# A batch's routing next to its layer norm in the first stage, and two bias additions on GpSimd in the middle stage

## The chip, the cores and the metric

One Trainium2 chip, one core. The metric is the time of one execution in microseconds on the device; a kernel's time is the median over its runs. All data are float32. In the profile PE is TensorE (PEld its weight loads), DVE is VectorE, ACT is ScalarE, POOL is GpSimd, and SP is SyncE, which only issues DMAs (SPq is its queue).

## The reference

The input x has 8 batches of 1024 tokens of 256 features. Three blocks follow each other, each with a residual: a feed-forward block taken by half, attention, and the same feed-forward block once more with the same weights.

```python
x = x + 0.5 * ffn(layernorm(x))
x = x + attn(layernorm(x))
x = x + 0.5 * ffn(layernorm(x))

def ffn(x):                      # 16 experts, inner size 128; shared expert of 2 x 128
    s    = softmax(x @ gate_w.T)             # 16 scores, plus gate_b for the choice
    keep = best 2 of 4 groups of experts     # by the sum of a group's two best
    w, idx = best 2 experts within keep      # w: the scores of the chosen
    y = sum over the 2 of  w * ((silu(x @ We1 + be1) * (x @ We3 + be3)) @ We2 + be2)
    z = (silu(x @ ws1 + bs1) * (x @ ws3 + bs3)) @ ws2 + bs2      # shared expert
    return y + z

def attn(x):                     # linear attention, 16 heads of 16
    q, k, v = split(x @ w_qkv.T);  q, k = relu(q), relu(k)
    z   = 1 / (sum over tokens of k, times q, + eps)
    out = ((v^T k) q) * z
    return out @ w_proj.T + b_proj
```

Two biases matter here: `bs2`, which the kernel keeps halved and broadcast as `hb2`, and `b_proj`, kept as `bpj`. Each is a row of 256 that is added to every token.

## The kernel before

One batch of x is a tile of 128 partitions by 8 x 256 (NT = 8 token tiles); NB = 2 halves of HT = 4 token tiles each. The work has five stages.

1. **First stage, 0 to about 249 us.** For rounds r = 0 to 8: `normed(0, r)` makes the layer norm of batch r (statistics L253 on DVE, scaling L270 on ACT) and transposes it (L283 on PE, copies L286 on ACT). `route(…, r-1)` routes the batch before: gating matmul L323 and transposes L332 on PE, a chain of some thirty small DVE operations from `sm` L339 over `sel` L406 to `cw` L433, in the middle of it the matmuls L416 (tile `prk`) that count tokens by expert, and then on POOL 16 indirect DMAs per batch (L467), which scatter the rows of tokens to the experts' lists `xs_d` in DRAM, with small `L456` and `L461` operations among them. `shared_units(r-2)` computes the shared expert of the batch two back: hidden layer L796 on PE (tiles `p_s`), L800 on ACT, L801 on DVE; output L815 on PE (`py_s`) and L819 on DVE, which adds to x. `add_bias` (L806, DVE) adds `hb2` to half a batch of x first.
2. **Expert blocks of the first feed-forward layer, about 249 to 522 us**, in a written-out order: rows `xg` are loaded by SP from `xs_d` (L654), transposed (L678, tile `pxg`), run through the experts (L699 to L731) and scattered to `ys_d` by POOL (L736). The routing of batch 7, beyond its first two steps, and parts of the shared expert of batch 7 (`late`) run behind these blocks. In between, x tiles are moved to and from `xk_d` in DRAM.
3. **Middle stage, about 522 to 1000 us.** In round r: `begin(r)` adds the experts' outputs to x (`combine`, L856 on DVE, operands loaded by SP) and makes the layer norm for attention; `attention(r-1)` adds `bpj` to the whole batch (L867, DVE, 128 x 2048), then q and k (L877, L881, L882), the sums `pgs` (L885), `gk` (L892, ACT), `dg` (L896, DVE), `pks` (PE), `ksb` (L905, ACT), `qk` (L920, DVE) and `den`, and the projection `pp` (L954, PE), which L958 on DVE adds to x; `finish(r-2)` makes the second feed-forward block's layer norm and routing, with scatters again on L467. The shared expert of that block is computed here for the last batches only.
4. **Expert blocks of the second feed-forward layer, about 1000 to 1271 us**, as in 2.
5. **The end, to 1376 us**: shared expert and output of the remaining batches, with `add_bias` on DVE as in the first stage.

The order: the engines run their own instruction streams, each in order. In stages 1, 3 and 5 a scheduler places each engine's instructions; it gives precedence to what is emitted first. The emission is by Python generators, and `run` takes one step of each in turn:

```python
run(normed(0, r), routing, shared_units(xs[s], xnTs.pop(s), f"s0_{s}"))   # s = r - 2
```

In the last two rounds this differs: in round 7 the routing of batch 6 is run alone before the others; in round 8 only two steps of batch 7's routing are run. `xpool` holds 4 batches of x at a time, so batches 0 to 4 (all but the last LATE = 3) are stored to `xk_d` as they finish. In the middle stage x is loaded again, and from batch 3 on this is done by SP one round ahead.

SP issues the loads of expert weights and rows in order. One of the loads, of the experts' output biases (L236), uses a buffer that the shared expert's last hidden matmul must have left; the first `xg` load of the expert blocks stands behind it.

Of the kernel before, what the change touches and what calls it, by code (L numbers as in the profile page):

```python
# [15 lines left out]
ALU = mybir.AluOpType  # L16
# [3 lines left out]
P = 128  # L20
# [6 lines left out]
def macaron_kernel(  # L27
# [18 lines left out]
    nc = tc.nc  # L46
    B, N, D = x.shape
# [4 lines left out]
    NT = N // P  # L52
# [4 lines left out]
    NB = N // TB  # L57
# [9 lines left out]
    HT = TPB  # L67
# [38 lines left out]
    def load_x(b, src, pieces=1):  # L106
        xt = xpool.tile([P, NT, D], F32, tag="x", name=f"x_{b}")
        n = NT // pieces
        for i in range(pieces):
            nc.sync.dma_start(  # L110
                out=xt[:, i * n : (i + 1) * n, :], in_=src[:, i * n : (i + 1) * n, :]
            )
        return xt

    xs = {0: load_x(0, x_v[0], 4)}
# [17 lines left out]
    hb2 = const.tile([P, D], F32, name="hb2")  # L133
    nc.sync.dma_start(out=hb2[:], in_=bs2.partition_broadcast(P))
    nc.vector.tensor_scalar(hb2[:], hb2[:], 0.5, None, ALU.mult)
    bpj = const.tile([P, D], F32, name="bpj")
# [22 lines left out]
    def ramp(n, first, step, name):  # L159
# [36 lines left out]
        base=0, channel_multiplier=1,  # L196
# [21 lines left out]
    def half(tag, shape, name, dtype=F32):  # L218

        if tag == "xnT":  # L220
            n = shared_room["turn"] % NXT
            shared_room["turn"] += 1
            if n < NXT - NXT_KEPT:
                return shared_room["pool"].tile(
                    shape, dtype, tag=tag, name=name, bufs=NXT - NXT_KEPT
                )
            return big.tile(shape, dtype, tag=tag, name=name, bufs=NXT_KEPT)
        return big.tile(shape, dtype, tag=tag, name=name, bufs={"xn": 8, "k": 2}[tag])
# [80 lines left out]
    def new_base(which):  # L309
        base = rp.tile([P, E], F32, tag="base", name=f"base_{which}", bufs=2)  # L310
        nc.gpsimd.tensor_copy(base[:], eoff[:])
        return base
# [167 lines left out]
    def counts(base, name, unit):  # L480

        cnt = rp.tile([1, E], F32, tag="cnt", name=f"cnt_{name}", bufs=2)
        nc.vector.tensor_tensor(cnt[:], base[0:1, :], eoff[0:1, :], ALU.subtract)
        nc.vector.tensor_scalar(cnt[:], cnt[:], 1.0 / unit, None, ALU.mult)
        return cnt

    def whole(cnt, name, op):

        more = half("xn", [1, E, MB], f"more_{name}")
        nc.vector.tensor_tensor(  # L490
            more[:], cnt[:].unsqueeze(2).to_broadcast([1, E, MB]),
            iblk[0:1, 0:MB].unsqueeze(1).to_broadcast([1, E, MB]), op,
        )
        nblk = rp.tile([1, E], F32, tag="nb", name=f"nb_{name}")
        nc.vector.tensor_reduce(nblk[:], more[:], axis=AX.X, op=ALU.add)
        return nblk
# [48 lines left out]
    def first_map(base, which):  # L545


        name = f"{which}a"
        cnt = counts(base, name, RB)
        nc.vector.tensor_scalar(cnt[:], cnt[:], -1.0, None, ALU.add)  # L550
        nblk = whole(cnt, name, ALU.is_ge)
        maps = []
        for _ in listed(nblk, None, name, maps, RB):
            pass
        end = rp.tile([1, E], F32, tag="done", name=f"done_{name}", bufs=2)
        nc.vector.tensor_tensor_scan(end[:], ones[0:1, 0:E], nblk[:], 0.0, ALU.mult, ALU.add)
        nc.vector.tensor_tensor(end[:], end[:], nblk[:], ALU.subtract)
        nc.vector.tensor_scalar(end[:], end[:], -1.0, float(N1), ALU.mult, ALU.add)
        nc.vector.tensor_scalar(end[:], end[:], 0.0, None, ALU.max)
        nc.vector.tensor_tensor(end[:], end[:], nblk[:], ALU.min)  # L560
        nc.vector.tensor_scalar(end[:], end[:], float(NR), None, ALU.mult)

        fill = half("xn", [P, DR], f"fill_{which}")
        nc.gpsimd.memset(fill[:], 0.0)
        nc.gpsimd.memset(fill[:, D : D + 1], float(SKIP))
        return maps, end, fill
# [27 lines left out]
    def behind(routing, base, which, maps, done, fill):  # L594

        for _ in range(7):
            next(routing)
            yield
        other = second_map(base, which, maps, done)
        last = next(other)  # L600
        yield
        fills = fill_up(last, fill)
        live = True
        while live:
            live = False
            for g in (routing, routing, other, fills):
                if next(g, StopIteration) is not StopIteration:
                    live = True
                    yield
# [192 lines left out]
            h[:], p3[:], bc[:, NS + s : NS + s + 1], h[:], ALU.add, ALU.mult  # L802
        )

    def add_bias(xh):
        nc.vector.tensor_tensor(  # L806
            xh, xh, hb2[:].unsqueeze(1).to_broadcast([P, HT, D]), ALU.add
        )

    def outputs(xh, hs, name):  # L810
# [17 lines left out]
    def half_of(xt, nb):  # L828
        return xt[:, nb * HT : (nb + 1) * HT, :]

    def shared_units(xt, xnT, name, late_bias=False):
        for nb in range(NB):
            xh = half_of(xt, nb)
            if not late_bias:
                add_bias(xh)
            hs = []
            for s in range(NS):
                if late_bias and nb == 0:
                    hs.append(spare(f"hs_{name}_{nb}_{s}"))
                else:  # L840
                    hs.append(
                        mid.tile([P, TB], F32, tag="u2", name=f"hs_{name}_{nb}_{s}", bufs=3)
                    )
                hidden(xnT[nb], s, hs[s], f"{name}_{nb}")
                yield
            if late_bias:
                add_bias(xh)
            yield from outputs(xh, hs, f"{name}_{nb}")

    def combine(which, b, xt):  # L850

        for j in range(0, NT, 2):
            for k in range(K):
                y = mid.tile([P, 2, D], F32, tag="u1", name=f"y_{which}_{b}_{j}_{k}", bufs=4)
                nc.sync.dma_start(out=y[:], in_=ys_v[k, b, :, j : j + 2, :])
                nc.vector.tensor_tensor(  # L856
                    xt[:, j : j + 2, :], xt[:, j : j + 2, :], y[:], ALU.add
                )
            yield


    def attention(b, xt, axn, axnT):
# [1 line left out]
        pgs = [  # L864
            ps_h.tile([P, D + 1], F32, tag="p3", name=f"pgs_{b}_{c}") for c in range(NC)
        ]
        nc.vector.tensor_tensor(  # L867
            xt[:], xt[:], bpj[:].unsqueeze(1).to_broadcast([P, NT, D]), ALU.add
        )
        for j in range(NT):  # L870
            nb, t = divmod(j, HT)
            if t == 0:
# [88 lines left out]
    def part(gen, n):  # L961

        for _ in range(n):
            next(gen, None)
            yield

    def run(*gens):

        live = [g for g in gens if g is not None]
        while live:  # L970
            for g in list(live):
                if next(g, StopIteration) is StopIteration:
                    live.remove(g)

    xns, xnTs = {}, {}

    def normed(which, b):

        xns[b], xnTs[b] = [], []
        parts = NT // 2 if (which, b) == (0, 0) else 1  # L980
        yield from layernorm(xs[b], f"f{which}_{b}", xns[b], DR, parts)
        yield from transposed(xns[b], f"f{which}_{b}", xnTs[b])


    LATE = 3
    base = new_base(0)
    for r in range(B + 1):
        if r == 1:
            load_late_weights()
        if 2 <= r + 1 < B:  # L990
            xs[r + 1] = load_x(r + 1, x_v[r + 1])
        s = r - 2
        routing = None
        if r >= 1:
            routing = route(base, 0, r - 1, xns.pop(r - 1), xnTs[r - 1], r == B)
        if r == B:
            maps, done, fill = first_map(base, 0)
            steps = behind(routing, base, 0, maps, done, fill)
        if r == B - 1:
            run(routing)  # L1000
        run(
            normed(0, r) if r < B else None,
            routing if r < B else part(routing, 2),
            shared_units(xs[s], xnTs.pop(s), f"s0_{s}") if s >= 0 else None,
        )
        if 0 <= s < B - LATE:
            nc.sync.dma_start(out=xk_d[s][:], in_=xs.pop(s)[:])
    tc.no_sync_barrier()

    def park(b, j):  # L1010
# [22 lines left out]
        moves += [partial(fetch, b, j) for j in range(NT)]  # L1033

    s = B - 1
    late = shared_units(xs[s], xnTs.pop(s), f"s0_{s}", True)
    blocks(maps, 0, steps, by_block(moves), partial(steps_of, late, NS))
    for b in range(B - LATE, B - 1):
        xs.pop(b)
# [4 lines left out]
    base = new_base(1)  # L1044
    axns, last = {}, []

    def begin(b):
        yield from combine(0, b, xs[b])
        axns[b] = ([], [])
        yield from layernorm(xs[b], f"a{b}", axns[b][0], D + 1)  # L1050
        yield from transposed(axns[b][0], f"a{b}", axns[b][1])
# [15 lines left out]
    for r in range(B + 2):  # L1067
        if LATE <= r + 1 < B - 1:
            xs[r + 1] = load_x(r + 1, xk_d[r + 1])
        s = r - 3  # L1070
# [11 lines left out]
    s = B - 1  # L1082
# [6 lines left out]
    xh, hs, left, todo = {}, {}, {}, list(range(2, B - LATE))  # L1089
# [35 lines left out]
    maps, done, fill, routing = last  # L1125
# [49 lines left out]
    with tc.manual_schedule():  # L1175
# [10 lines left out]
        for h in range(NH):  # L1186
# [8 lines left out]
            b, nb = own[h]  # L1195
# [68 lines left out]
```

## Time and profile before

| | |
|---|---|
| median of 6 runs | 1371.29 us (1360.54 to 1384.53) |
| the profiled execution | 1377.62 us, span 1375.9 us, granted clock 0.941 |
| PE busy | 1184.0 us, 86% of the span |
| DVE busy | 885.8 us, 64% |
| POOL busy | 581.5 us, 42% |
| ACT busy | 540.4 us, 39% |
| scatters L467 on POOL | 256, mean 1031 ns |
| `hb2` adds L806 on DVE | 32 in the kernel, 128 x 1024, median 1218 ns |
| `bpj` adds L867 on DVE | 8, 128 x 2048, median 2277 ns |

The shares are means over stages that differ, so the view of slices and the windows of one stage matter more than the totals. Idle time of an engine is listed under the group that came after it, with what ended it. POOL in particular idles for long stretches in the middle stage, waiting for the routing weights `cw` (L433).

### The profile page before, as it was taken

The page shows a single profiled execution, that of the slowest core. Times are in us where ns is not written, and L with a number is a line of the kernel's source. Part 1 is how long each engine was busy: PE and PEld are TensorE (multiplying, and loading weights), DVE is VectorE, ACT ScalarE, POOL GpSimd, SP SyncE. Part 2 cuts the span into 40 slices and gives each one's busy share as a digit, 9 for nine tenths or more (in the row PEclk, how much of TensorE's full clock was granted, in tenths as well). Part 3 has the DMA queues.
Part 4 walks back from the last instruction along what each step waited for, and adds up shares of the span by engine and source line. Part 5 has one row for each costly group of instructions (what it writes and reads, how often), then busy time and mean ns, then how long its engine had stood idle before and what let it go on. Part 6 is the DMA issues. An engine that isn't in the chain of part 4 may idle for free. (4 is left out here: it accounts for less than half of the span.)

```text
span 1375.9 us, 20671 instructions
## 1 busy us (share of the span) xinstructions
PE 1184.0 (86%) x5728; PEld 851.7 (62%) x5728; DVE 885.8 (64%) x2878; ACT 540.4 (39%) x1120; POOL 581.5 (42%) x719
## 2 busy tenths in 40 slices
PE   7898767688888988998878879899897879898998
PEld 3554444576778874665655556556576668786555
DVE  6787537576556567766757748627686545665587
ACT  6566422222235542464454454542432223553110
POOL 1566555266665551004152253250536666555010
PEclk9999989799999998999889979999999999999999
DMA  9335323456665535533352330010435555552996
GB/s 352 141 133 175 127 75 108 146 186 186 195 188 168 165 110 181 172 138 121 111 186 97 120 124 32 33 63 5 152 118 172 187 181 176 159 155 84 333 372 242
DMA packets 96101, 212.20 MB, mean 154 GB/s; under 512 B 17381, under 2 KB 45290, under 8 KB 92272
## 3 DMA queue, kind: packets, MB, share of 16 engines
q1 hardware_dynamic: 68288, 134.77, 30.6%
q0 software_dynamic: 27696, 76.07, 14.9%
q8 instruction: 49, 0.80, 0.2%
q14 instruction: 68, 0.56, 0.1%
HBM read 110.75 MB, written 102.64 MB: 155 GB/s over the span
## 5 line engine op out<-in xcount | busy, mean ns | idle before, releaser
L736 POOL DMA_INDIRECT ys_d<-yo,at x276 | 276.9, 1003 | 236.7 <-DVE rest L731 171.9
L699 PE MATMUL q<-xgT,wc 128*128 128x128 f32 (+1 forms) x1568 | 286.2, 332 | 65.4 <-ACT xgT L683 36.9
L467 POOL DMA_INDIRECT xs_d<-xn_f,rowi x256 | 263.8, 1031 | 110.1 <-issue 60.9
L699 PEld LDWEIGHTS q<-xgT,wc 128*128 128x128 f32 x1568 | 233.7, 197 | 93.7 <-ACT xgT L683 46.1
L683 ACT COPY xgT<-pxg 128x512 f32<-128x512 f32 x138 | 81.3, 590 | 281.4 <-PE pxg L678 115.0
L796 PE MATMUL p_s<-xnT_f,ws_sb 128*128 128x512 f32 x352 | 166.1, 611 | 1.1 <-ACT hs_s L800 1.1
L706 DVE SCALAR_TENSOR_TENSOR hb<-q,wc,hb 128x128 f32<-128x128 f32 (+1 forms) x196 | 73.5, 400 | 138.0 <-PE q L699 52.7
L731 DVE CUSTOM_DVE_ANT_0 yo<-qy,b2c,at 128x256 f32<-128x256 f32 x276 | 122.8, 482 | 47.9 <-PE q L699 7.0
L725 PE MATMUL qy<-wall,hb 128*128 x552 | 145.7, 387 | 6.0 <-DVE rest L731 6.0
L815 PE MATMUL py_s<-ws_sb,hs_s 128*128 128x256 f32 x512 | 131.4, 400 | 20.0 <-DVE hs_s L801 14.5
L815 PEld LDWEIGHTS py_s<-ws_sb,hs_s 128*128 128x128 f32 x512 | 98.0, 198 | 56.3 <-DVE hs_s L801 23.7
L877 PE MATMUL pk<-wqk_sb,xnT_a 128*128 128x512 f32 x256 | 126.5, 612 | 0.5 <-ACT q L882 0.2
L461 POOL TENSOR_SCALAR xn_f<-cw 128x4 f32<-128x4 f32 x64 | 15.8, 254 | 255.3 <-DVE cw L433 252.4
L800 ACT ACTIVATE hs_s<-p_s,bc 128x512 f32<-128x512 f32 x64 | 43.7, 687 | 182.8 <-PE p_s L796 131.7
L725 PEld LDWEIGHTS qy<-wall,hb 128*128 128x128 f32 x552 | 102.8, 195 | 20.1 <-issue 5.1
L796 PEld LDWEIGHTS p_s<-xnT_f,ws_sb 128*128 128x128 f32 x352 | 67.8, 198 | 66.3 <-issue 61.2
L705 ACT ACTIVATE hb<-q,wc 128x128 f32<-128x128 f32 (+1 forms) x196 | 75.2, 420 | 74.0 <-PE q L699 35.3
L678 PE MATMUL pxg<-ident,xg 128*128 128x128 f32 x552 | 84.4, 277 | 11.1 <-DMA xg<-xs_d 11.1
L678 PEld LDWEIGHTS pxg<-ident,xg 128*128 128x128 f32 x552 | 70.1, 143 | 25.6 <-DMA xg<-xs_d 11.5
L801 DVE SCALAR_TENSOR_TENSOR hs_s<-p_s,bc,hs_s 128x512 f32<-128x512 f32 x64 | 47.6, 745 | 58.4 <-PE p_s L796 39.6
L885 PE MATMUL pgs<-xn_a,k 128*128 128x257 f32 x256 | 72.6, 401 | 8.3 <-issue 4.8
L796 PE MATMUL p_s<-xnTr,ws_sb 128*128 128x512 f32 x160 | 70.4, 593 | 0.3 <-PEq L786 0.3
(302 smaller groups left out, 1743.2 us busy)
## 6 DMA issues: line engine op xcount, KB each, us to landing
xg<-xs_d SPq DMA_DIRECT2D x80, 264.0 KB
y<-ys_d SPq DMA_DIRECT2D x64, 256.0 KB
y<-ys_d SPq DMA_DIRECT2D x32, 512.0 KB
xg<-xs_d SPq DMA_DIRECT2D x116, 132.0 KB
xk<-x SPq DMA_DIRECT2D x8, 1024.0 KB
x<-xk SPq DMA_DIRECT2D x8, 1024.0 KB
wall<-in_wexp_dram SPq DMA_DIRECT2D x4, 1540.0 KB
x<-in_x_dram SPq DMA_DIRECT2D x6, 1024.0 KB
```

The costliest lines, as they stand in the source:

```text
L467: nc.gpsimd.indirect_dma_start(out=v[:, :], out_offset=bass.IndirectOffsetOnAxis(ap=rowi[:, j, k : k + 1], axis=0), in_=xn[:, t, :], in_of ...
L678: nc.tensor.transpose(pt[:, c, s * P : (s + 1) * P], xg[i][:, s, c * P : (c + 1) * P], ident[:],)
L683: nc.scalar.copy(xgT[i][:], pt[:])
L699: nc.tensor.matmul(pt_[:, cs], w[:, s, o + c * P : o + (c + 1) * P], t[:, c, cs], start=(c == 0), stop=(c == NC - 1),)
L705: nc.scalar.activation(h[:, cs], p1[:, cs], AF.Silu, bias=w[:, s, W2 - 2 : W2 - 1])
L706: nc.vector.scalar_tensor_tensor(h[:, cs], p3[:, cs], w[:, s, W2 - 1 : W2], h[:, cs], ALU.add, ALU.mult)
L725: nc.tensor.matmul(py[:, s : s + 1, :], h[:, s * P : (s + 1) * P], w2s[s % len(w2s)], start=True, stop=True,)
L731: nc.vector.tensor_tensor_reduce(out=yo[:, s, :], in0=py[:, s, :], in1=b2c[s % len(w2s)][:, 0, :], scale=a[:, s, 1:2], scalar=0.0, op0=ALU ...
L736: nc.gpsimd.indirect_dma_start(out=ys_views[i * NR + s][:, :], out_offset=bass.IndirectOffsetOnAxis(ap=a[:, s, 0:1].bitcast(I32), axis=0), ...
L796: nc.tensor.matmul(pt[:], w[:, c, s * P : (s + 1) * P], xnT[:, c, :], start=(c == 0), stop=(c == NC - 1),)
L815: nc.tensor.matmul(py[:, t - t0, :], hs[s][:, t * P : (t + 1) * P], ws2_sb[:, s, :], start=(s == 0), stop=(s == NS - 1),)
L877: nc.tensor.matmul(pk.rearrange("p k d -> p (k d)"), tile_of(axnT, c, j), wqk_sb[:, c, :], start=(c == 0), stop=(c == NC - 1),)
```

## The change

It has two parts.

**Order in the first stage.** A new generator `routed(b)` emits the layer norm of batch b and its routing one after the other, so in round r both belong to batch r; the shared expert remains two batches back. `weave` takes five steps of `routed` and then two of the shared expert in turn. Batch 7's routing is split as before (two steps, the rest behind the expert blocks), but the split is inside `routed`, in round 7, and round 8 holds only the shared expert of batch 6.

**The two biases.** `shared_units` of the first feed-forward block no longer adds `hb2` to x, neither in the first stage nor, for batch 7, behind the blocks. Instead `begin(b)` adds it in the middle stage, on GpSimd, half by half, ahead of `combine`. `attention` adds `bpj` on GpSimd too, in two halves. The second feed-forward block's `hb2` additions stay on DVE.

```diff
-    def add_bias(xh):
-        nc.vector.tensor_tensor(
-            xh, xh, hb2[:].unsqueeze(1).to_broadcast([P, HT, D]), ALU.add
+    def add_bias(xh, bias=hb2, engine=nc.vector):
+        engine.tensor_tensor(
+            xh, xh, bias[:].unsqueeze(1).to_broadcast([P, HT, D]), ALU.add
         )
...
-    def shared_units(xt, xnT, name, late_bias=False):
+    def shared_units(xt, xnT, name, bias=True, late=False):
...
-            if not late_bias:
+            if bias:
                 add_bias(xh)
...
-            if late_bias:
-                add_bias(xh)
             yield from outputs(xh, hs, f"{name}_{nb}")
...
# attention
-        nc.vector.tensor_tensor(
-            xt[:], xt[:], bpj[:].unsqueeze(1).to_broadcast([P, NT, D]), ALU.add
-        )
+        for nb in range(NB):
+            add_bias(half_of(xt, nb), bpj, nc.gpsimd)
...
+    def weave(many, few):
+        run(many and groups(many, 5), few and groups(few, 2))
+
+    def groups(gen, n):
+        live = True
+        while live:
+            for _ in range(n):
+                live = live and next(gen, StopIteration) is not StopIteration
+            if live:
+                yield
...
+    def routed(b):
+        yield from normed(0, b)
+        if b == B - 1:
+            begun["maps"] = first_map(base, 0)
+        routing = route(base, 0, b, xns.pop(b), xnTs[b], b == B - 1)
+        if b == B - 1:
+            begun["routing"] = routing
+            routing = part(routing, 2)
+        yield from routing
...
-        routing = None
-        if r >= 1:
-            routing = route(base, 0, r - 1, xns.pop(r - 1), xnTs[r - 1], r == B)
-        if r == B:
-            maps, done, fill = first_map(base, 0)
-            steps = behind(routing, base, 0, maps, done, fill)
-        if r == B - 1:
-            run(routing)
-        run(
-            normed(0, r) if r < B else None,
-            routing if r < B else part(routing, 2),
-            shared_units(xs[s], xnTs.pop(s), f"s0_{s}") if s >= 0 else None,
+        weave(
+            routed(r) if r < B else None,
+            shared_units(xs[s], xnTs.pop(s), f"s0_{s}", False) if s >= 0 else None,
         )
...
+    maps, done, fill = begun["maps"]
+    steps = behind(begun["routing"], base, 0, maps, done, fill)
...
-    late = shared_units(xs[s], xnTs.pop(s), f"s0_{s}", True)
+    late = shared_units(xs[s], xnTs.pop(s), f"s0_{s}", False, True)
...
# begin
+        for nb in range(NB):
+            add_bias(half_of(xs[b], nb), hb2, nc.gpsimd)
         yield from combine(0, b, xs[b])
```

Counted over the kernel, DVE issues 16 additions of 128 x 1024 and 8 of 128 x 2048 fewer, and POOL 32 additions of 128 x 1024 more, all of them in the middle stage.

More of the change, by code (lines that the diff above doesn't have):

```diff
@@ L837, in shared_units @@
             for s in range(NS):
-                if late_bias and nb == 0:
+                if late and nb == 0:
                     hs.append(spare(f"hs_{name}_{nb}_{s}"))
@@ L986, in macaron_kernel @@
     base = new_base(0)
+    begun = {}
+    def routed(b):
[7 more added lines that the diff above has]
+        yield from routing
     for r in range(B + 1):
```

## The prediction, made before the change was run

> **What bounds the kernel now.** I read the page's forty slices first, to find stages in which TensorE is not full.
>
> ```profile
> PE   7898767688888988998878879899897879898998
> DVE  6787537576556567766757748627686545665587
> POOL 1566555266665551004152253250536666555010
> ```
>
> One slice is 34.4 us. PE is the fullest engine nearly everywhere; the holes that concern the change are slices 5 to 8 (the second half of the first stage) and slices 21 to 24 (in the middle stage). Next, the windows of the first stage: the columns are the busy us of PE, PEld, DVE, ACT and POOL, then clock and DMA.
>
> ```profile
> 160.00:170.00 10.00, 8.51 (x56) 4.35 (x54) 3.00 (x12) 7.41 (x13) 7.82 (x8) 1.00 0.48 180
> 170.00:180.00 10.00, 5.87 (x22) 3.64 (x21) 5.36 (x18) 0.79 (x2) 7.71 (x11) 1.00 0.32 117
> 180.00:190.00 10.00, 6.11 (x18) 3.10 (x17) 6.32 (x17) 1.27 (x2) 1.40 (x4) 0.80 0.07 27
> 190.00:200.00 10.00, 6.59 (x51) 3.76 (x50) 0.00 (x0) 3.55 (x6) 7.60 (x8) 0.84 0.27 96
> 240.00:250.00 10.00, 1.05 (x5) 1.05 (x6) 0.81 (x5) 0.00 (x0) 3.52 (x4) 0.53 0.67 236
> ```
>
> No engine is full here: the rounds are held by chains between engines. The last row is the stage's end, and the chain of waits names what ends it (us in total, times, longest):
>
> ```profile
> ACT hs_s L800 <- PE p_s L796: 42.3, 10, 9.2
> PE pxg L678 <- DMA xg<-xs_d: 11.1, 1, 11.1
> DVE sm L339 <- PE pg L332: 13.7, 4, 10.8
> PE prk L416 <- DVE sel L406: 8.4, 4, 3.6
> ```
>
> The shared expert ends at 237.9; the last batch's scatter on POOL ends near 246; the first expert transpose (L678) starts at 248.95, after 11.1 us of nothing on PE.
>
> Then the middle stage's timeline, one round. POOL first:
>
> ```profile
> 711.12 0.96 POOL L467 DMA_INDIRECT xs_d<-xn_f,rowi  x1 [0.30 <-issue]
> 712.10 0.20 POOL L456 IOTA xn_f<- 128x32 f32 x1
> 741.90 0.41 POOL L461 TENSOR_SCALAR xn_f<-cw 128x4 f32<-128x4 f32 x2 [28.23 <-DVE cw L433]
> ```
>
> POOL is busy with 16 scatters from 690.5 and then idles 28 us. DVE in the same round:
>
> ```profile
> 708.02 1.29 DVE L856 TENSOR_TENSOR x<-x,y 128x512 f32<-128x512 f32 x2 [4.13 <-DMA x<-xk]
> 713.77 0.29 DVE L896 TENSOR_SCALAR dg<-ident,gk 128x128 f32<-128x128 f32 x1 [4.46 <-ACT gk L892]
> 716.66 1.23 DVE L920 TENSOR_TENSOR qk<-q,ksb 128x1024 f32<-128x1024 f32 x1 [0.54 <-ACT ksb L905]
> ```
>
> dg and qk open the attention's second half: PE has holes from 692 to 720 and is full from 717 to 747. The middle rounds are 54 us apart (POOL's scatters start at 690.5 and 744.4).
>
> **First stage.** Each round holds three things: a batch's layer norm, the routing of one batch, the shared expert of another. Before, the routing is one batch behind its layer norm; after, both are of one batch, placed five steps to two ahead of the shared steps. No PE work is added or removed. Two numbers follow.
>
> Length of a round, by the routing's prefix matmuls (prk, L416), at 35.4, 65.75, 95.6, 123.2, 155.1, 186.3 and 217.35: a mean of (217.35 - 35.4) / 6 = 30.3 us. In the instruction order, 16 pairs of p_s matmuls stood ahead of each prk, 12 in the last two rounds, mean 14.7; after, 13, 15, 11, 12, 15, 10, 13: over the last six 12.7. Shared work is 16 p_s pairs of 0.86 us and 16 py pairs of 0.43, 20.6 us a batch, so two pairs of sixteen fewer take 2.6 us from each round: 27.7. Off DVE go the 14 hb2 adds (L806, 1.22 us), 2.4 us a round. If DVE was also on the round's chain, both count: 25.3. If the chain from layer norm to prk, now in one piece, sets the round, nothing is gained: 30.3. I take 27.7, by the PE content, since DVE still idles in these windows (3.0 to 6.3 of 10). The first prk loses four adds, 35.4 - 4 = 31.5.
>
> The tail: what leaves the rounds must be done after prk 6: 23 p_s pairs (19.8) and 30 py pairs (12.9), with batch 7's transposes and gating (about 5): 37.7, against some 16 us to the last p_s before. But the scatter (16 at 1.28, 20.5 us) now ends under that work, and the wait of 11.1 shrinks to the expert loads behind L236 on SP, which is queued until the last p_s, and the 2.8 us that xg took from issue (246.12) to pxg: about 6 in all. So the first pxg is at prk 6 + 43.5. With 27.7: 31.5 + 166 + 43.5 = 241, **8 us gained**. Bounds: 227 (22 gained) with 25.3; 257 (8 lost) with 30.3.
>
> **Middle stage, what DVE loses.** Eight bpj adds (L867, 128x2048, 2.28 us each, 18.2 us) and two late hb2 adds (2.4 us near 526.8).
>
> **Middle stage, what POOL gains.** 32 adds of 128x1024 f32. No such add is in the trace. Nearest rows on POOL: memsets, 0.33 us for 264 columns against 0.10 for 4, 0.9 ns a column, so 1.0 us for 1024; the affine select, 0.35 for 128 columns against 0.23 for 16, 1.07 ns, so 1.3 us with one input. An add reads two: 2.3 us as the sum of a select and a memset, which I take; ends 1.0 (one pass) and 3.4 (three passes). The Trainium skill (GPSIMD Engine Reference, 3.1 Elementwise) measures 4497 ns for 2048 columns; that gives an estimate of 2.25.
>
> The bpj adds are needed only by the pp adds (L958) near 730, and POOL idles from 713.7 to 741.9: 4.6 us hidden. Without that cover they would delay the next scatter by 4.6. The hb2 adds are not hidden. Each must precede its half's combine (L856), and in POOL's order the adds of batches 5, 6 and 7 stand behind the 16 scatters of batches 0, 1 and 2. So the combine, at 708.02 before, waits for 712.3 + 2.3 = 714.6. Behind it on DVE, in order, stand dg, the sum sm of the routing, and qk. In DVE's order the add precedes dg: dg at 714.6 + 0.7 = 715.3 instead of 713.77, +1.5; then PE (pks), ACT (ksb) and qk are as late, and after them the saturated stretch, cw and the next scatter. Less the 2.28 of bpj: -0.8 for each of three rounds, if the engines don't touch each other.
>
> **They may.** Two POOL instructions beside a two-input add of DVE:
>
> ```profile
> 854.38 0.97 POOL L467 DMA_INDIRECT xs_d<-xn_f,rowi  x1 [0.30 <-issue]
> 855.44 1.23 DVE L806 TENSOR_TENSOR x<-x,hb 128x1024 f32<-128x1024 f32 x1 [1.26 <-issue]
> 855.66 1.86 POOL L467 DMA_INDIRECT xs_d<-xn_f,rowi  x1 [0.30 <-issue]
> 857.68 1.23 DVE L806 TENSOR_TENSOR x<-x,hb 128x1024 f32<-128x1024 f32 x1 [1.01 <-ACT xn_f L270]
> 857.82 1.17 POOL L461 TENSOR_SCALAR xn_f<-cw 128x4 f32<-128x4 f32 x1
> ```
>
> The scatter took 1.86 instead of 0.97, and the tiny L461, 0.22 elsewhere, took 1.17 and ended 0.08 after the add. The later of the two stood still. The Trainium skill (SBUF — State Buffer, Who interferes with whom) has the rule: a VectorE instruction with two inputs in that memory and a GpSimd instruction that reads it share a port, and "Whoever issues first gets the shared pair for the whole instruction". That speaks against the change; by that rule the middle stage's loss is the blocked case below, without it the free one.
>
> No row shows DVE waiting for POOL; bounds are 0 and one whole POOL add, 2.3 us, for each pair that meets. Blocked, in batches 5 to 7: the combine's add waits for the second hb2 add as well (+2.3 - 0.6 of waits that already overlap, dg at about 717), qk or its neighbour for a bpj add (+2.3): 1.5 + 1.7 + 2.3 + about 0.8 for a second such meeting = 6.3, less 2.28: +4.0, three rounds, 12 us. The other five rounds: a bpj add blocks one operation (2.3) and 2.28 is saved: 0. Batch 4, whose load lands at 607.3, pays its 2.3. The lead-in: six hb2 adds from 522.5 take 13.8 us, against combine's start at 529.7; +3.5, less the 2.4 of the late adds: 1.1. Sum 12 + 2.3 + 1.1 = **15 us lost**. Free: -0.8 x 3 - 2.28 x 5 - 2.4 = 16 gained. I take the blocked one, because the two rows above show an exclusive wait in the one direction; the other is not shown.
>
> Sum: -8 + 15 = +7 us on the profiled execution's 1377.62 (span 1375.9), which lies 6.3 above the median of the runs. On the median, 1371.29 + 7 = **1378 us**, +0.5%. A measurement of this kernel can tell about 1% (13.7 us) from no change, so this is within 1%.
>
> **Rivals.** *The chain of one batch sets the first stage's rounds* (slower). For it: layer norm, transposes, gating, top-k and prk follow each other, and DVE waits 13.7 us for pg already. Against it: PE's content between prks falls. Price: rounds of 30.3, 8 us lost instead of 8 gained, +23 in all: 1394. It decides from rounds of about 28.8 on (1.1 us over mine, six times, is the 6.7 that lacks to 1%).
>
> *The engines do not block each other* (faster). For it: no row shows DVE held by POOL, and the adds fall partly in stretches in which DVE waits anyway. Against: the pair above. Price: -8 - 16 = -24: 1347. Should the first stage's rounds not shorten with it, -8: 1363.
>
> *A later POOL takes the critical place*: if an add costs 3.4 us, 32 of them are 109 us, and each hb2 pair is 2.2 later: 3 x 2.2 + 2 = 9 more: 1387.
>
> **How the numbers follow.** Forecast (1366 to 1390 is its own range) 0.40; slow first stage 0.22; free engines 0.30; costly adds 0.08. Faster by over 1%: most of the free case and a sliver of the forecast, 0.26 + 0.03 = 0.29. Slower by over 1%: the slow stage 0.20, costly adds 0.06, the forecast's upper end 0.14: 0.40. The rest, 0.31, is within. The range leaves a tenth on either side: low 1340, a little under the free case, high 1402, a slow first stage with some of the costly adds.
>
> **What would show it.** Right: prk intervals near 27.7, the first pxg near 241 with no wait for xg of more than 3 us; in the middle, L856 waiting for POOL's L806 in three rounds, dg and qk 4 to 6 us later after the scatters, POOL's adds at 2.3 us or DVE's two-input ones longer than 0.69 and 1.23 beside them. Wrong: intervals of 30 or more (then the first rival), middle rounds of 52 us or less (the second), or POOL's add outside 1.0 to 3.4.

## The result and the profile after

The changed kernel takes 1417.91 us (median of 20 runs, 1400.76 to 1426.69) against 1370.52 for the kernel before (46 runs beside them): 1.0344 times as long, 95% interval 1.0317 to 1.0371, or 47 us. The forecast was 7 us. Its profiled execution took 1424.35 us, span 1422.2, 46.3 more than the span before. By the first expert transposes and the ends, the 46.3 lie as follows:

| stage | before | after | difference | forecast |
|---|---|---|---|---|
| start to first pxg (L678) | 248.95 | 266.85 | +17.9 | -8 |
| first pxg to the second layer's first pxg | 749.3 | 775.1 | +25.8 | +15 |
| from there to the end | 377.6 | 380.3 | +2.6 | 0 |

The page's slices, now 35.6 us each: PE is at 7 in the first six (213 us), and POOL's digits of slices 16 to 26 add up to 43 where they made 25.

```profile
PE   7777778797889996898687797899998779988998
DVE  6644557585556557848568476555867546655587
POOL 1655555165665555412643633640526665555000
```

The first stage in windows that each start at a prk (columns as in the prediction: PE, PEld, DVE, ACT, POOL). First the six rounds from prk 0 to prk 6, before and after, then the tail after the change, from prk 6 to the first pxg:

```profile
35.37:217.35 181.98, 150.46 (x672) 88.43 (x673) 119.64 (x403) 86.17 (x134) 108.33 (x141) 0.93 0.35 125
32.34:223.72 191.38, 142.93 (x618) 84.46 (x619) 105.87 (x388) 84.64 (x131) 103.61 (x141) 0.85 0.34 126
223.72:266.85 43.13, 37.63 (x160) 23.31 (x158) 22.86 (x53) 9.62 (x14) 18.32 (x24) 0.97 0.31 117
```

The tail is what was forecast (43.1 us, 87% of it PE work). The rounds aren't. Work did leave them: 54 matmuls fewer, PE busy 7.5 us less (1.3 a round, where 2.6 were forecast, with the granted clock at 0.85 instead of 0.93), VectorE busy 13.8 us less. And yet the six rounds take 191.4 us instead of 182.0; the longest, from 60.44 to 96.47, takes 36. The chain of waits of the first stage, lines that answer to those shown before; the first is that of gT before the change:

```profile
ACT gT L328 <- remote: 8.7, 3, 4.5
ACT hs_s L800 <- PE p_s L796: 46.5, 13, 9.2
ACT gT L328 <- remote: 20.3, 4, 8.4
DVE sm L339 <- PE pg L332: 16.5, 3, 9.3
PE prk L416 <- DVE sel L406: 14.7, 6, 7.4
PE pxg L678 <- DMA xg<-xs_d: 5.3, 1, 5.3
```

The wait for xg has halved, as forecast. The waits on the routing's chain have grown: sm from 13.7 to 16.5, prk from 8.4 to 14.7, and gT (L328) from 8.7 to 20.3. "Remote" means that the profile found no instruction whose end fits the release. gT, the copy of the gating scores, waits for a semaphore that in the trace PE alone raises, and the ends of matmuls are modelled in these profiles: the wait is for PE's gating matmuls.

The middle stage, timeline of the round that answers to the one shown before. DVE:

```profile
751.24 2.82 DVE L854 TENSOR_TENSOR x<-x,y 128x512 f32<-128x512 f32 x1 [8.43 <-POOL x L806]
753.98 2.37 DVE L893 TENSOR_SCALAR dg<-ident,gk 128x128 f32<-128x128 f32 x1
758.14 2.36 DVE L917 TENSOR_TENSOR qk<-q,ksb 128x1024 f32<-128x1024 f32 x2
```

POOL beside it:

```profile
747.63 0.97 POOL L467 DMA_INDIRECT xs_d<-xn_f,rowi  x1 [0.30 <-issue]
748.84 4.67 POOL L806 TENSOR_TENSOR x<-x,hb 128x1024 f32<-128x1024 f32 x2
753.70 2.57 POOL L806 TENSOR_TENSOR x<-x,bpj 128x1024 f32<-128x1024 f32 x1 [0.20 <-ACT xn_a L270]
```

POOL's adds start when its last scatter has been issued. The combine (L854) waits 8.43 us for the first add, and then takes 2.82 us instead of 0.69: it ends half a microsecond after the second add, at 754.06. dg takes 2.37 instead of 0.28 and ends when the bpj add does; the prediction had qk "or its neighbour" there. The two qk (one line, 2.36 together) are not held. This is the blocked case of the prediction.

### The profile page after: what moved, and what is told of

It is laid out like the page before. It is cut to its first block, busy times and chain, and to the rows that moved or that the text cites. A ratio compares the mean times of both kernels' runs of the same rounds, so it can differ in the third digit from the quotient of the medians.

```text
span 1422.2 us, 20691 instructions
## 1 busy us (share of the span) xinstructions
PE 1201.7 (84%) x5728; PEld 861.7 (61%) x5728; DVE 889.7 (63%) x2854; ACT 540.4 (38%) x1119; POOL 656.1 (46%) x751
## 5 line engine op out<-in xcount | busy, mean ns | idle before, releaser
L736 POOL DMA_INDIRECT ys_d<-yo,at x276 | 275.8, 999 | 242.7 <-DVE rest L731 176.6
L699 PE MATMUL q<-xgT,wc 128*128 128x128 f32 (+1 forms) x1568 | 284.9, 330 | 62.1 <-ACT xgT L683 34.4
L796 PE MATMUL p_s<-xnT_f,ws_sb 128*128 128x512 f32 x352 | 171.0, 623 | 0.0
L815 PE MATMUL py_s<-ws_sb,hs_s 128*128 128x256 f32 x512 | 136.0, 414 | 25.4 <-DVE hs_s L801 19.5
L815 PEld LDWEIGHTS py_s<-ws_sb,hs_s 128*128 128x128 f32 x512 | 104.1, 209 | 62.9 <-DVE hs_s L801 28.3
L725 PEld LDWEIGHTS qy<-wall,hb 128*128 128x128 f32 x552 | 104.3, 198 | 20.7 <-issue 7.4
L678 PE MATMUL pxg<-ident,xg 128*128 128x128 f32 x552 | 84.7, 278 | 5.3 <-DMA xg<-xs_d 5.3
L678 PEld LDWEIGHTS pxg<-ident,xg 128*128 128x128 f32 x552 | 70.6, 144 | 20.3 <-DMA xg<-xs_d 5.7
L819 DVE SCALAR_TENSOR_TENSOR x<-py_s,x 128x512 f32<-128x512 f32 x56 | 38.0, 687 | 67.6 <-PE py_s L815 33.4
```

The source lines that it names most:

```text
L678: nc.tensor.transpose(pt[:, c, s * P : (s + 1) * P], xg[i][:, s, c * P : (c + 1) * P], ident[:],)
L699: nc.tensor.matmul(pt_[:, cs], w[:, s, o + c * P : o + (c + 1) * P], t[:, c, cs], start=(c == 0), stop=(c == NC - 1),)
L725: nc.tensor.matmul(py[:, s : s + 1, :], h[:, s * P : (s + 1) * P], w2s[s % len(w2s)], start=True, stop=True,)
L736: nc.gpsimd.indirect_dma_start(out=ys_views[i * NR + s][:, :], out_offset=bass.IndirectOffsetOnAxis(ap=a[:, s, 0:1].bitcast(I32), axis=0), ...
L796: nc.tensor.matmul(pt[:], w[:, c, s * P : (s + 1) * P], xnT[:, c, :], start=(c == 0), stop=(c == NC - 1),)
L815: nc.tensor.matmul(py[:, t - t0, :], hs[s][:, t * P : (t + 1) * P], ws2_sb[:, s, :], start=(s == 0), stop=(s == NS - 1),)
```

## The experiments

Runs that were made together share a chip. The kernel before takes 1368 to 1392 us on most chips used here, but 1243 on one, so a kernel is held against runs on its own chip; where that isn't possible, the text says so. Stage times are each from one profiled execution; one and the same first stage gave a first pxg of 242.7 to 249.0 in five runs (before, before_again, bpj_alone, beside, beside_write) and of 256.9 on another chip, that of the changed kernel 260.8 to 266.9 in four (after, after_again, after_dve, after_third), and the old order without the hb2 adds 250.3 to 258.2 in three (biases_alone, hb2_alone, hb2_dve).

The theory at the outset: the two parts add up, the first stage loses by its order, the middle stage by GpSimd; against it, that one part is good and its interplay with the other costs.

**The two parts, alone.** The new order with all biases where they were; both biases moved with the old order; and each bias moved alone. The edits are those of the change, undone in part:

```diff
# order_alone: begin() without hb2, attention() with the old L867, shared_units(..., bias=True)
# biases_alone: run(normed(0, r), routing, shared_units(..., False)) as before
# hb2_alone: as biases_alone, with the old L867;  bpj_alone: kernel before with
-        nc.vector.tensor_tensor(xt[:], xt[:], bpj..., ALU.add)
+        for nb in range(NB):
+            add_bias(half_of(xt, nb), bpj, nc.gpsimd)
```

> The first stage's new order alone, all biases on VectorE and in their old places. Theory A (the two halves of the change add up; the first stage's loss is the order's): prk intervals of about 31.5 to 33 us, first pxg near 267 to 270 (the hb2 adds are back), the middle stage as before, the whole 16 to 22 us longer than before, near 1390. Theory B (the order is good, and it is the missing adds that let the scheduler place other work badly): first pxg at or under 249, the whole not longer than before.

Measured: 1.006 times before (1.0027 to 1.0093), about 8 us, first pxg 254.4. Neither theory has it: the loss is half of Theory A's, and there is one.

> Both biases on GpSimd in the middle stage, the first stage in its old order without the hb2 adds. Theory A: first pxg 243 to 249 (the adds were hardly on the first stage's path), the middle stage about 25 us longer, the whole about 20 to 27 us longer, near 1395. Theory B: first pxg late as after the change, 260 or more, and the whole 40 us longer.

Measured: 1.0234 (1.0178 to 1.0291), 32 us; first pxg 251.6. This lies between the theories.

> Only hb2 moved to GpSimd in the middle stage; bpj stays one VectorE add of 128x2048, order of before. Theory A1 (hb2 is the dear one, since the combine waits for it and it queues on GpSimd): middle stage 18 to 25 us longer, the round of batch 2 and 3 without the 14 us wait of the combine, because no bpj stands ahead of hb2 in GpSimd's queue. Theory A2 (the two biases hurt each other by the queue): middle stage only 5 to 12 us longer.

Measured: 1.0272 (1.0198 to 1.0345), 38 us; first pxg 258.2. From there to the second layer's first pxg it takes 774.7 us, 25.6 more than order_alone, whose middle stage is the old one; Theory A1 said 18 to 25. But the combine still came late without any bpj in the queue: dg to dg of the round of batch 4 took 42.7 us, against 39.5 in order_alone.

> Only bpj moved to GpSimd, in two halves; hb2 as before. Theory A1: GpSimd idles 28 us a round and nothing waits for bpj before pp, VectorE is relieved of 18 us: between 8 us shorter and 4 longer than before. Theory A2 (each GpSimd add holds VectorE's operations for its 2.4 us, 16 of them): 5 to 15 us longer.

Measured: 1.007 (1.0031 to 1.0109), 10 us: Theory A2.

So most of the loss comes with hb2's move, which takes it out of the first stage and puts it on GpSimd. Order and biases about add up: 1.006 and 1.0234 make 1.029, a little under the 1.034 of the whole. The two biases alone, 1.0272 and 1.007, make more than both together, within the intervals. In the first stage each part loses: on this chip the first pxg is at 242.7 with the old first stage (bpj_alone), at 254.4 with the new order, at 251.6 and 258.2 without the hb2 adds. The relief of DVE by 18 us through bpj brought nothing; moving it cost 10. No part is a gain.

**Is it GpSimd or the place?** hb2 in the middle stage on VectorE (old order), and the whole change with both biases on VectorE:

```diff
-            add_bias(half_of(xs[b], nb), hb2, nc.gpsimd)
+            add_bias(half_of(xs[b], nb), hb2, nc.vector)
```

> hb2 moved to the middle stage as in hb2_alone, but on VectorE. Theory L or Q (GpSimd is what costs): at most 10 us longer than before, at least 15 us shorter than hb2_alone. Theory M (the move itself costs, since in the middle stage the combine starts the path and the first stage did not need the relief): 20 us or more longer than before, near hb2_alone.

Measured: 1.0101 (1.0046 to 1.0156), 14 us; 24 us less than on GpSimd by the two ratios, which are of two chips. GpSimd costs as Theories L and Q say, but the move by itself costs more than their 10.

> The changed kernel, unchanged, a second profile: its stages are the measure for the two runs beside it. First pxg within 5 us of the 266.85 of its first profile if the first stage's loss is no accident of one execution; near 250 if it is.

Measured: first pxg 260.8; it is no accident of one execution. The middle stage's rounds again: 330.7 us from the first pxg to the first dg and 380.2 from there to the last batch's dg, where an unchanged kernel (before_again below, on another chip) has 321.2 and 359.7.

> The changed kernel with both biases on VectorE, in the same places of the middle stage. Theory L (GpSimd's adds cost by blocking VectorE and by waiting in its queue): the middle stage 15 us or more shorter than after the change, the whole about 20 to 25 us over before, that is order (+8) and the moved hb2 (+14). Theory M (the places cost, not the engine): no more than 8 us shorter than after the change. The first stage is the same program in both, so first pxg near 267 under both.

Measured: 1.0127 (1.0053 to 1.02), 17 us. The same two stretches take 324.5 and 359.4. From the first pxg to the second layer's first pxg it is 747.0 us, where after_again on the same chip takes 772.8: 25.8 us less, with VectorE doing 32 more adds. That is the whole loss of this stage (before_again, on the other chip, takes 744.1). Here the engine is the cost. What remains is about the first stage's: first pxg 264.6, where beside_write, with the old first stage, has 244.0 on this chip.

> The kernel before, unchanged, on this chip: its stages are the measure for the runs beside it. All theories expect the same stages as in the first profile, within about 2%.

Measured: 1370.25 us, first pxg 246.4, and the two stretches just given.

**What of GpSimd costs: its queue, or VectorE's standing still?** The kernel before, with as many added elements on GpSimd on data nobody needs; then the same with writes only.

```diff
+    def beside(name):                       # called in begin() and attention()
+        for i in range(4):
+            t = mid.tile([P, 2, D], F32, tag="u2", ...)
+            nc.gpsimd.tensor_tensor(t[:], <hb2 broadcast>, <bpj broadcast>, ALU.add)
# beside_write:                  for _ in range(3): nc.gpsimd.memset(t[:], 1.0)
```

> The kernel before, with 64 additional GpSimd adds of 128x512 (as many elements as after the change), on data that nobody needs; VectorE does all it did before. Theory L (port lock: GpSimd's adds hold VectorE's two-input operations): the combine adds and others grow from 0.69 to 1 us and more where they meet, the middle stage gets 8 to 25 us longer. Theory Q (only the queue and the data dependence cost): VectorE's durations unchanged, the middle stage within 3 us of before.

Measured: 1.0399 (1.0354 to 1.0444), 54 us for work that nobody waits for, twice what Theory L expected. All 64 adds ran between 522 and 626 us, and the loss lies there: 25.6 us before the first dg and 23.0 between the first two batches' dg, against before_again. Groups by shape between 515 and 660 us, where these adds were placed (columns: count, busy us, mean ns, idle before); in the run of the kernel before, the first two means were 681 and 688, the fourth 2286:

```profile
L864 DVE TENSOR_TENSOR xf<-xf,y 128x512 f32<-128x512 f32 x24 | 34.4, 1451 | 0.1
L864 DVE TENSOR_TENSOR x<-x,y 128x512 f32<-128x512 f32 x14 | 17.2, 1261 | 11.4 <-DMA x<-xk 11.3
L253 DVE BATCH_NORM_STATS2 st_a<-xf 128x6 f32<-128x256 f32 x24 | 9.2, 396 | 0.0
L875 DVE TENSOR_TENSOR xf<-xf,bpj 128x2048 f32<-128x2048 f32 x3 | 8.9, 2964 | 0.0
```

Operations with two inputs in SBUF take 1.3 to 2.1 times as long; the statistics with one input stay at 396. That is not all of the 54: pgs waited once 17.3 us for a small memset of xn_a that stood behind these adds in POOL's queue, so here the queue costs too.

> As the run with idle adds beside the kernel before, but GpSimd only writes: 192 memsets of 128x512, about as much GpSimd time, no read of SBUF. Theory L (two-input operations of VectorE and GpSimd's reads exclude each other): the combine adds back at 0.69 us, and what remains over before is the queue in front of the small memsets of xn_a, under 20 us. Theory Q (it is GpSimd's queue or its time, whatever it does): about as long as with the adds, 45 us or more over before.

Measured: 1.0045 (1.0003 to 1.0086), 6 us, with 94.5 us of memsets. The same groups:

```profile
L862 DVE TENSOR_TENSOR xf<-xf,y 128x512 f32<-128x512 f32 x24 | 16.0, 679 | 3.1 <-DMA y<-ys_d 3.1
L862 DVE TENSOR_TENSOR x<-x,y 128x512 f32<-128x512 f32 x12 | 7.9, 689 | 15.2 <-DMA x<-xk 11.3 <-DMA y<-ys_d 3.8
L903 DVE TENSOR_SCALAR dg<-ident,gk 128x128 f32<-128x128 f32 x2 | 6.3, 6064 | 0.6 <-ACT gk L899 0.6
```

The two-input adds are back at 0.68. So it is GpSimd's reading that holds them; nearly as much GpSimd time that only writes (94.5 us, where the adds took 102.5) costs little. The last line is a miss of Theory L as I had written it: dg, a one-input TENSOR_SCALAR of 0.28 us, stood still for 6.2 us while a dozen memsets passed, one after the other, so writes exclude this form.

**What sets the first stage's rounds?** First, the kernel before without the shared expert of batches 0 to 6:

```diff
-            shared_units(xs[s], xnTs.pop(s), f"s0_{s}") if s >= 0 else None,
+            None,
```

> The kernel before without the shared expert of batches 0 to 6 in the first stage (it leaves that part of the sum out). Theory C (PE's content between the prks sets the rounds, as the prediction took it): 20.6 of 30.3 us of work gone, so prk intervals fall to what GpSimd's 16 scatters need, 23 us or less. Theory D (the chain transposes, gating, softmax, top-k, prk sets the round, and the shared expert only fills its gaps): intervals stay at 28 us or more. In between, 24 to 28: the chain is near that long and the shared work stretches it by waits in the engines' queues.

Measured: intervals of 27.4 us on average, the case between the theories; first pxg 222.8. In the stretch of the six rounds (PE first):

```profile
28.53:192.79 164.26, 40.97 (x318) 28.15 (x319) 83.99 (x349) 50.91 (x96) 105.05 (x141) 0.55 0.46 167
```

PE is busy a quarter of the time, and six rounds take 164 us instead of 179 (the kernel before on the same chip). 20.6 us of PE work less in a round bring 2.4 us. By that slope the forecast's 2.6 us of content are worth 0.3. One reserve: the granted clock falls too, from 0.94 in these rounds of before_again to 0.55 (the third number from the end), so the matmuls that are left may run slower. For the rest I split the six rounds at pgT (L323) and pg (L332), by the starts in PE's timeline; chips differ from row to row, the last four rows share one:

| sum of six rounds, us | prk to pgT | pgT to pg | pg to prk | all |
|---|---|---|---|---|
| before, first profile | 30.3 | 23.8 | 127.8 | 182.0 |
| after, first profile | 34.5 | 32.3 | 124.6 | 191.4 |
| order_alone | 26.9 | 24.6 | 135.9 | 187.4 |
| after_dve | 31.7 | 30.0 | 125.5 | 187.2 |
| weave_1_2 | 32.2 | 34.4 | 124.8 | 191.5 |
| before_third | 25.5 | 23.2 | 139.6 | 188.3 |
| after_third | 30.9 | 30.8 | 127.8 | 189.5 |
| pe_only_second | 52.9 | 52.5 | 79.9 | 185.3 |
| bare_second | 46.9 | 57.2 | 67.9 | 172.0 |

The third link is VectorE's top-k chain. After the change 14 adds of 1.22 us are off VectorE, and the link is 3 us shorter (12 on the last chip), while the first two are 12.7 longer (13). Summed over the six third links by VectorE's timeline, its work on shared operations falls from 33.6 to 20.7 us, but its idle time right before them rises from 22.1 to 33.5 (on the last chip from 33.0 to 21.4 and from 30.6 to 35.7). Does content in the tail then come free when it is put back into the rounds?

```diff
-        run(many and groups(many, 5), few and groups(few, 2))
+        run(many and groups(many, 1), few and groups(few, 2))   # biases on VectorE
```

> As the changed kernel with both biases on VectorE, but the weave takes one step of the routing and two of the shared expert in turn, so that the engines' orders leave 16 instead of 23 p_s pairs and 24 instead of 30 py pairs behind prk 6: 8.6 us less in the tail, 1.4 us more in each round. Theory D (the chain sets the rounds, shared work fills its gaps): prk 6 stays within 3 us of 218, the tail falls from 46 to about 37, first pxg 253 to 257. Theory C (PE's content sets the rounds): prk 6 moves to about 226, first pxg stays near 264.

Measured: prk 6 at 223.5, tail 41.1, first pxg 264.7, the whole 1.0198 (1.0114 to 1.0282). This is Theory C's pxg: with 8.6 us of content more in the rounds, prk 6 is 5.3 later than in after_dve, though that ran on another chip. Yet hb2_dve, on this chip, whose orders leave the same counts behind prk 6, has prk 6 at 213.4 and pxg at 250.3. So at the same amount of shared work the two orders differ by 10 us in six rounds: the amount alone doesn't set them. That it matters where in the chain the work stands is my reading.

Through which engine? PE's shared matmuls kept (on other operands of the same shapes), ScalarE's and VectorE's part left out, in both orders:

```diff
-            shared_units(xs[s], xnTs.pop(s), f"s0_{s}") if s >= 0 else None,
+            matmuls_alone(xnTs.pop(s), f"s0_{s}") if s >= 0 else None,
```

> The kernel before with the shared expert's matmuls of batches 0 to 6 kept on PE (on other operands of the same shapes) and everything that ScalarE and VectorE do for it in the first stage left out. Theory V (VectorE's queue stretches the chain: between pg and prk it takes 20.8 us a round, 11.8 without shared work, because shared operations that wait for PE stand in it): pg to prk falls to 12 to 14 us a round although PE does all its work, and rounds to 27 or less. Theory P (PE's queue: the chain's matmuls wait behind shared matmuls): pg to prk stays at 18 us or more, rounds at 29 or more.

Measured: pg to prk 11.7 us a round, rounds 24.0, first pxg 219.5, on the chip on which the kernel before takes 1243 us: nothing to hold the rounds against there.

> The same in the changed kernel: PE's shared matmuls kept, the shared expert's work on ScalarE and VectorE left out of the first stage. Theory V: pg to prk 12 to 14 us a round, rounds 27 or less, first pxg 15 us or more earlier than the 261 to 267 of the changed kernel. Theory P: rounds stay near 31, first pxg within 8 us of it.

Measured: pg to prk 11.1 us, rounds 23.6, first pxg 229.8, same chip. The comparison was made again with all four on one chip, one profile each:

> The kernel before, unchanged: the measure for the three runs beside it. All theories: pg to prk about 20 us a round if the chip is like the first ones.

Measured: 1398.44 us, first pxg 256.9, pg to prk 23.3 us a round.

> The changed kernel, unchanged. All theories: first pxg 12 to 18 us later than in the kernel before beside it, middle stage 24 to 29 us longer.

Measured: 1431.21 us, first pxg 265.0 (8 later, less than I expected), the middle stage 25 us longer.

> PE's shared matmuls kept, the shared expert's work on ScalarE and VectorE left out of the first stage, order before. Theory V (VectorE's queue stretches the chain): pg to prk within 3 us a round of the run without any shared work, and 6 us or more under the kernel before. Theory P (PE's queue): within 3 us a round of the kernel before.

Measured: pg to prk 13.3 us a round: Theory V for this link, though ScalarE's part is left out as well, so its queue isn't told apart from VectorE's. But the rounds are 30.9, hardly shorter than 31.4: the first two links took up what the third gave. The first pxg, at 264.2, is 7 us later than in the kernel before.

> No shared expert of batches 0 to 6 in the first stage (that part of the sum is left out): the chain by itself. Both theories: pg to prk near 12 us a round.

Measured: pg to prk 11.3 us, rounds 28.7, first pxg 231.1.

No run that does all of the work beat the kernel before, and none pointed to a version that would.

## Why the prediction was wrong

**The POOL add** was priced at 2.3 us; alone it takes 2.35 (the shortest of each group 2.34 to 2.35), beside VectorE up to 2.9. Right, and with it the estimate from the Trainium skill's 4497 ns for 2048 columns (GPSIMD Engine Reference, 3.1 Elementwise).

**They block each other**: right, and now shown in the direction that no row of before showed. The larger of the combine's two groups between 500 and 1000 us, before and after:

```profile
L856 DVE TENSOR_TENSOR x<-x,y 128x512 f32<-128x512 f32 x40 | 26.9, 686 | 25.8 <-DMA x<-xk 22.9 <-DMA y<-ys_d 2.8
L854 DVE TENSOR_TENSOR x<-x,y 128x512 f32<-128x512 f32 x40 | 46.2, 1166 | 43.3 <-POOL x L806 41.5 <-DMA y<-ys_d 1.6
```

The other 24 adds go from 683 to 1102 ns. Together that is 29 us for the 64 adds; qk, dg and den add 3.0, 2.5 and 4.8. That is 40 us more on VectorE, against 20.6 taken off it in this stage (18.2 of bpj, 2.4 of the late hb2 adds). The Trainium skill's rule (SBUF — State Buffer, Who interferes with whom) on two-input VectorE operations and GpSimd reads agrees with the pair of runs with adds (54 us) and with memsets (6 us).

**Batches 5 to 7, 4 us each, 12 in all**: measured from one batch's first dg to the next +7.5, +0.1 and +4.1, 11.7 in all. Right in sum, not round by round; that the sum fits so closely is in part luck. The last four stretches, 0 forecast, sum to -0.7: right.

**The lead-in and batch 4** are the mis-sized terms of this stage: 1.1 and 2.3 forecast, 7.2 and 7.6 measured. In the lead-in I had counted the six hb2 adds as 13.8 us in front of a combine that begins 7 us later, and no blocking. That difference is 6.6; the +3.5 in the sum was not worked out from it. It also went another way: the combine began on the first batch while the adds of the next ran, each at 2.6 us, 3.2 us earlier after the first pxg than before, but from there to the first dg it took 53.3 us instead of 42.9. Nine of its adds took 1.1 to 2.8 us in place of 0.68, 14 us more.

For batch 4 I had priced the add alone. POOL and DVE in this round:

```profile
633.10 2.36 POOL L806 TENSOR_TENSOR xf<-xf,bpj 128x1024 f32<-128x1024 f32 x1 [20.88 <-ACT xn_a L270]
635.42 4.68 POOL L806 TENSOR_TENSOR x<-x,hb 128x1024 f32<-128x1024 f32 x2
637.81 6.79 DVE L854 TENSOR_TENSOR x<-x,y 128x512 f32<-128x512 f32 x4 [14.25 <-POOL x L806]
```

The hb2 adds stood behind a bpj add that had waited 20.9 us. It looks as if GpSimd's queue made the combine late, but the batch's load landed only at 634.8 (then end POOL's and VectorE's waits for it), so the queue held the hb2 add for 0.6 us. The 7.6 are these: the load came 2.5 us later after the previous dg, which no run here explains; the combine began 3.0 us after it instead of at once (the queue and one add); and then it took 2.1 more, two of its adds 2.8 us each. hb2_alone, with no bpj in the queue, has 42.7 us for this round and biases_alone beside it 44.5; in biases_alone the queue holds the hb2 add for 0.5, and most of the rest is a second add of the combine that takes 2.8 us, beside the bpj add behind the hb2 adds.

**The first stage's rounds** are the step that failed: 27.7 us forecast, 31.9 measured, six times 4.2, or 25 us of the 39 that separate 46 from 7. The step was that PE's content between two prks sets the round. It was taken from how much PE work stands there, and not from what ended the waits. The content did fall, and the rounds grew; by bare_before content is worth about an eighth of itself, with the reserve of the lower clock. The other reading in the prediction, that L806 on VectorE might be 2.4 us a round of the chain, fell as well: between pg and prk VectorE waits in its queue for shared operations that wait for PE, and in the first profiles 12.9 us less of work let it wait 11.4 us longer. Taking out all shared work of VectorE and ScalarE shortens that link, from 23.3 to 13.3 us.

**Rival 1** had the mechanism, one batch's chain sets the rounds, but a price at 30.3 that was the kernel's own round and so no loss in the rounds; in the first profile the six rounds have become 9.4 us longer: 4.2 to pgT and 8.5 from pgT to pg, less 3.2 from pg to prk. A single round makes 6.9 of the 8.5: pg starts 10.3 us after pgT where it was 3.4, and in the other three runs with this first stage 9.5 to 10.7, with no work shown on PE, ScalarE and VectorE; in bare_before it is 10.2 too, and in the two runs on the chip of the 1243 us no such link is over 4.5. In the first profile after the change the modelled end of this round's last gating matmul lies at 70.9, and PE's semaphore releases gT at 79.7. What holds PE's result so long is open, and so is what bounds the rounds of 27 to 29 us with no shared work; the granted clock of TensorE is low there (0.55), but as cause or effect no run tells.

**The tail and its start** were right: first prk 31.5 forecast, 32.3 measured; 43.5 from prk 6 to pxg, 43.1 measured; the wait for xg 11.1 to 5.3, near the sum's 6 in all, though over the 3 named as a sign. The 11.5 us by which the tail grew were to be paid by shorter rounds, and weren't. One attribution was wrong: order_alone's tail is 31.6 with 7 p_s pairs, so the new order alone pushes no work into it; the missing hb2 adds do (hb2_dve: 36.9, 16 pairs), and both together make it 43. The scheduler's order hangs on operations that seem to have nothing to do with it.

**Rivals 2 and 3** didn't occur: the middle rounds were 56 us, and a POOL add stayed under 3.4 (2.9 at most). The 2.6 us at the end of the kernel, where nothing was changed, were not looked into.

## What to carry to other kernels

Before moving an elementwise operation to GpSimd because it idles, look at what VectorE does at that time: if it reads two operands from SBUF, GpSimd's reading is not beside it but in front of it, and the cost is counted on VectorE. What is queued behind the moved operation can count as well: in one run a small memset behind such adds came 17 us late. And a busy share, however high, isn't a bound: a round's length is read from the chain of waits, and leaving the supposed bound out is the cheapest experiment.

## What the runs showed of the hardware

GpSimd's own adds slow down too: 1.62 us on average for 128x512 beside VectorE, 1.26 at the least. A chain of GpSimd instructions can keep one VectorE instruction out over many of them: dg waited through a dozen memsets of 0.53 us. And the chips differ: the kernel before, 1368 to 1392 us on four of them, took 1243 in its one run on a fifth.
